# The second self-attention on one ring of double PSUM banks, with its group of heads in another order

## The chip, the cores and the metric

The kernel runs on one core of one Trainium2 chip. The metric is the device time of one execution in microseconds, as the median of several runs. Before the change it is 2383.0 us (three runs: 2380.41, 2383.2 and 2383.0).

## The reference

Two transformer blocks follow each other over x of 8 batches x 512 tokens x 256 channels in float32. The first block has self-attention, cross-attention and a gated feed-forward, all with 16 heads of 16 channels. The second has self-attention with 16 heads of 64 channels, cross-attention to 64 context tokens and a feed-forward with gelu. The change is in the second block's self-attention alone:

```python
def _attn(xq, ctx, wq, wkv, wo, bo):
    q = _heads(xq @ wq)
    k, v = jnp.split(ctx @ wkv, 2, axis=-1)
    ...
    q = _rope(q, sq, cq)
    k = _rope(k, sk, ck)
    sim = jnp.einsum('bhnd,bhmd->bhnm', q, k) * DH ** (-0.5)
    a = jax.nn.softmax(sim, axis=-1)
    o = jnp.einsum('bhnm,bhmd->bhnd', a, v)
    o = o.transpose(0, 2, 1, 3).reshape(xq.shape[0], xq.shape[1], MID)
    return o @ wo + bo
...
attn_in = _adaln(x, cond, ln1_w, ln1_b, g1_w, g1_b, b1_w, b1_b)
x = _attn(attn_in, attn_in, sa_wq, sa_wkv, sa_wo, sa_bo) + x
```

`_rope` multiplies the even and odd channels by a cosine and a sine table and adds or subtracts the products. The 16 heads of 64 channels make 1024 columns for each of q, k and v.

## The kernel before

**Work of a batch.** A batch has 512 tokens. Its normalised rows are transposed into `hT` (two tiles of 128 channels x 512 tokens). Its 16 heads are taken in four groups `g` of four. For a group, `turned` (L999) projects the even and the odd channels of four heads (two products of 128 x 512, each over two slices of 128 channels), multiplies each by the cosine and the sine table on VectorE (L1007, L1008) and lets GpSimd form the rotated even and odd halves (L1010, L1011). It is called for queries and for keys; its products lie in four buffers with the tag `t`, which each call uses all. `values` (L989) projects v for half of the heads (512 columns), tile by tile of 128 tokens.

**Scores and values.** Keys are taken in four tiles of 128 tokens. `score(g, kt)` (L1019) makes the scores of four heads for one key tile, for 512 queries: a head's even and odd halves are 32 rows each, so four heads stand side by side in the array as tiles of 32 rows x 128 columns, and each adds two products. Two double banks take them, and ScalarE makes two tiles `p` of exponentials from them (L1028; six buffers). `value(g, kt)` (L1030) multiplies `p` with v, in tiles of 128 rows x 64 columns, two heads side by side; bank O holds one pair of heads and bank D the other, over the four key tiles. ScalarE copies both to `oT` at the end. The sums of `p` over the key tiles are added up in `sm`: the first addition on GpSimd (L1043) and two more on VectorE (L1047), for each of two pairs of heads. `sums` (L1057) adds `sm` over the partitions with a matrix of ones in tiles of 128 x 32; ScalarE copies the result, and it goes to DRAM and back as `rec`, is inverted on VectorE (`inverse`, L1073), goes to DRAM and comes back spread over the partitions as `rb`. `scaled` (L1090) multiplies `oT` by `rb` on GpSimd. `out_tiles` (L1095) projects the 1024 channels back to 256 and VectorE adds the result to x.

A float32 product is two passes of TensorE in the trace; the profile counts passes.

**PSUM.** Eight banks of 512 float32 columns: two double banks S for scores, one bank O, one bank D, and two banks X for all else. S, O, D and X are rings of their own, so a projection waits for a projection's reader and scores for an exponential.

**Order.** TensorE, VectorE, ScalarE and GpSimd take their instructions in the order in which the Python code issues them (`manual_schedule`). DMAs are issued from SP, in the last group from ScalarE's queue. `slots` (L1152) runs over pairs of key tiles: the scores of an odd key tile, then the jobs listed for this slot (`steps`: projections of the next group or batch, an output projection), the scores of the next even tile, the values of the two tiles before it, then what is listed in `after` (sums, transposes). `mid` puts sums or inverses between jobs. So a group of four key tiles is spread over two slots. After the last group the projections of the cross-attention's values (`cross_values`, L964) run while the last sums go to DRAM and back.

Of the kernel before, what the change touches and what calls it, by code (L numbers as in the profile page):

```python
# [18 lines left out]
P = 128  # L19
# [68 lines left out]
def fast_path(ctx: ExitStack, tc: tile.TileContext, a: dict, out: bass.AP):  # L88
# [7 lines left out]
    psum = ctx.enter_context(tc.tile_pool(name="psum", bufs=2, space=bass.MemoryType.PSUM))  # L96
    turns, extra = [0], []

# [865 lines left out]
    def cross_values(wk, p):  # L964
        ps = bank_x()
        for k in range(2):
            mm(ps, cross["v"][:, k, p * P : (p + 1) * P], ctxzT[:, k, :], k == 0, k == 1)
        v = wk.tile([P, N], F32, tag=f"k{p % 2}", name="v")
        nc.scalar.copy(v, ps)
        nc.sync.dma_start(v_d[:, p], v.rearrange("p (b t) -> p b t", b=B))  # L970


    with tc.tile_pool(name="ph4", bufs=2) as wk:
# [3 lines left out]
        steps, mid, after = {}, {}, {}  # L977

        def last(slot, fn):
            steps.setdefault(slot, []).append(fn)  # L980

        def batch4(b):
            s = {}
            base = 2 * NG * b

            def turn():
                s["hT"] = transposed(nk, s["z"], b, a1, b1, 1)

            def values(half, ts):  # L989
                if ts[0] == 0:  # L990
                    s["v", half] = wk.tile([P, NT, 512], F32, tag="v", name="v")
                for t in ts:
                    ps = bank_x()
                    for k in range(2):
                        mm(ps, s["hT"][:, k, t * P : (t + 1) * P], w_sv[:, k, half * 512 : (half + 1) * 512],
                           k == 0, k == 1)
                    nc.scalar.copy(s["v", half][:, t, :], ps)

            def turned(g, w, tag, pss=None):  # L999

                even, odd = pss or (bank_x(), bank_x())
                for e, ps in enumerate((even, odd)):
                    for k in range(2):
                        mm(ps, w[:, k, (2 * g + e) * P : (2 * g + e + 1) * P], s["hT"][:, k, :], k == 0, k == 1)
                ec, es, oc, os = (wk.tile([P, N], F32, tag="t", name="t", bufs=4) for _ in range(4))
                for ps, c, sn in ((even, ec, es), (odd, oc, os)):
                    nc.vector.tensor_tensor(c, ps, rope_c, ALU.mult)  # L1007
                    nc.vector.tensor_tensor(sn, ps, rope_s, ALU.mult)  # L1008
                s[tag, g] = r = [wk.tile([P, N], F32, tag=f"{tag}{e}", name=f"{tag}{e}") for e in range(2)]
                nc.gpsimd.tensor_tensor(r[0], ec, os, ALU.subtract)  # L1010
                nc.gpsimd.tensor_tensor(r[1], es, oc, ALU.add)  # L1011

            def queries(g, pss=None):
                turned(g, w_sq, "q", pss)

            def keys(g, pss=None):
                turned(g, w_sk, "k", pss)

            def score(g, kt):  # L1019
                pss = [bank_s() for _ in range(2)]  # L1020
                for e in range(2):
                    for j in range(4):
                        r = slice(32 * j, 32 * j + 32)
                        mm(pss[j // 2][:, j % 2, :], s["k", g][e][r, kt * P : (kt + 1) * P], s["q", g][e][r, :],
                           e == 0, e == 1)
                for u in range(2):
                    s["p", g, kt, u] = pr = wk.tile([P, 2, N], F32, tag="p", name="p", bufs=6)
                    nc.scalar.activation(pr, pss[u], AF.Exp, scale=HD1 ** -0.5)  # L1028

            def value(g, kt):  # L1030
                if kt == 0:
                    s["o", 0], s["o", 1] = bank_o(), bank_d()
                for u in range(2):
                    p = 2 * g + u
                    for i in range(2):
                        lo = (p % 4) * P + 64 * i
                        mm(s["o", u][64 * i : 64 * i + 64, :], s["v", p // 4][:, kt, lo : lo + 64],
                           s["p", g, kt, u][:, i, :], kt == 0, kt == NT - 1)

                if kt == 0:  # L1040
                    for u in range(2):
                        s["sm", g, u] = sm = wk.tile([P, 2, N], F32, tag="sm", name="sm", bufs=4)
                        nc.gpsimd.tensor_tensor(sm, s["p", g, 0, u], s["p", g, 1, u], ALU.add)  # L1043
                if kt == 2:
                    for t in (2, 3):
                        for u in range(2):
                            nc.vector.tensor_tensor(s["sm", g, u], s["sm", g, u], s["p", g, t, u], ALU.add)  # L1047
                if kt == NT - 1:
                    for u in range(2):
                        s["oT", 2 * g + u] = o = wk.tile([P, N], F32, tag="oT", name="oT", bufs=10)  # L1050
                        nc.scalar.copy(o, s["o", u])


            def queue(g):
                return nc.scalar if (b, g) == (B - 1, NG - 1) else nc.sync

            def sums(g):  # L1057

                d = bank_x()
# [5 lines left out]
                queue(g).dma_start(dd, den.rearrange("(j r) n -> j r n", j=4)[:, 0, :])  # L1065
                if (b, g) != (B - 1, NG - 1):
                    sums_back(g)

            def sums_back(g):
                s["rec", g] = rec = wk.tile([P, 4 * N // P], F32, tag="rec", name="rec")  # L1070
                queue(g).dma_start(rec, flat(s["dd", g]))

            def inverse(g):  # L1073
                rec = s["rec", g]
                nc.vector.reciprocal(rec, rec)
                s["inv", g] = d = dram.tile([4, N], F32, tag="rec_d", name="rec_d")
                queue(g).dma_start(flat(d), rec)
                check(rec)
                if (b, g) != (B - 1, NG - 1):
                    inverse_back(g)  # L1080

            def inverse_back(g):
                d = s["inv", g]
                for u in range(2):
                    s["rb", g, u] = rb = wk.tile([P, N], F32, tag="rb", name="rb", bufs=3)
                    for e in range(2):
                        queue(g).dma_start(rb[64 * e : 64 * e + 64, :],
                                           d[2 * u + e : 2 * u + e + 1, :].to_broadcast([64, N]))

            def scaled(g, engines=None):  # L1090
                for u, eng in enumerate(engines or [nc.gpsimd] * 2):
                    o = s["oT", 2 * g + u]
                    eng.tensor_tensor(o, o, s["rb", g, u], ALU.mult)  # L1093

            def out_tiles(qp):  # L1095
                project_out(qp, lambda k: s["oT", k], w_so, 8, add_to(b))

            if b:

                pieces = normed_in_pieces(nk, b, EPS1, lambda z: s.update(z=z))  # L1100
                last(base - 8, pieces[0])
                last(base - 6, pieces[1])
                after[base - 6] = [pieces[2]]
                last(base - 5, lambda: add_row(b, row("sabo")))
                after.setdefault(base - 4, []).append(turn)
                last(base - 3, lambda: queries(0))
                last(base - 2, lambda: values(0, (0, 1)))
                last(base - 2, lambda: keys(0))
                last(base - 1, lambda: values(0, (2, 3)))
            else:  # L1110
                s["hT"] = ready

                def begin():
                    queries(0)
                    add_row(0, row("sabo"))
                    both = bank_s()
                    keys(0, (both[:, 0, :], both[:, 1, :]))
                    values(0, (0, 1))

                last(-1, begin)  # L1120

                after[-1] = [lambda: values(0, (2, 3))]
                last(4, lambda: [nc.gpsimd.memset(z, 0.0) for z in (kb, vb)])
                last(5, lambda: load_kb(0))
            for h in range(2):
                last(base + h, lambda h=h: values(1, (2 * h, 2 * h + 1)))
            for g in range(1, NG):
                last(base + 2 * g - 3, lambda g=g: queries(g))
                last(base + 2 * g - 2, lambda g=g: keys(g))
            tail = sums, sums_back, inverse, inverse_back, scaled, out_tiles  # L1130
            return score, value, sums, inverse, scaled, out_tiles, tail

        todo = [batch4(b) for b in range(B)]
# [1154 lines left out]
```

## Time and profile before

| What | Value |
|---|---|
| Median of three runs | 2383.0 us (2380.41 to 2383.2) |
| Span of the profiled execution, first to last instruction | 2378.6 us |
| Own time of the profiled execution outside that span | not listed; the median is 4.4 us above the span |
| Busy in the span: PE, DVE, POOL, ACT | 2361.7, 1141.8, 958.6, 886.8 us |
| Mean granted clock of TensorE | 0.998 |
| Second self-attention: from its first queries to the end of its last output projection | 828.1 to 1815.4 us |
| DVE additions of 128 x 1024 (L1047) | 128, mean 2026 ns, shortest 1211 ns |
| POOL additions of 128 x 1024 (L1043) | 64, mean 2370 ns |
| POOL rotations of queries (L1010, L1011) and of keys | mean 1866 and 2190 ns; 1273 and 1280 ns |
| DVE products with the tables (L1007, L1008), 128 x 512 | mean 690 and 680 ns |
| ACT exponentials of 128 x 1024 (L1028) | 256, mean 1021 ns |

The profile comes from one execution. PE is TensorE's matmul row, PEld its weight loads, which overlap it; DVE is VectorE, ACT ScalarE, POOL GpSimd, SP the queue that issues DMAs. A line of a group or of the timeline names the source line, the operation, the tile written and the tiles read, and the shape; for a matmul 128\*64 means 128 rows x 64 columns of the array. In the timeline the first number is the start and the second the length in us, merged over the instructions counted by x; in brackets stands how long the engine was idle before and who ended that. A matmul's end is modelled, so that matmuls that follow each other overlap a little; the distance of two starts says what a stretch takes.

### The profile page before, as it was taken

Reading aid. Unit: us, or ns where it says so; the run is one execution under the profiler, and the core shown is the slowest. Engines: PE = TensorE matmul, PEld = TensorE weight load, DVE = VectorE, ACT = ScalarE, POOL = GpSimd, SP = SyncE. Lnnn points to the kernel's source line nnn. Section 1 sums busy time; section 2 is a strip of 40 time slices with the busy share of each in tenths; the row PEclk is TensorE's granted clock in tenths of the full one; section 3 lists DMA queues with packets and bytes.
Section 4 is the critical chain, followed back from the end, with each engine's and each line's share of the span. In section 5 each row is a group of like instructions: output and inputs, shape, how many; then the busy total and the mean of one; then the engine's idle time right before and its main releaser. Section 6 shows DMA issues by size and latency. Waiting matters only on the chain.

```text
span 2378.6 us, 28548 instructions
## 1 busy us (share of the span) xinstructions
PE 2361.7 (99%) x10964; PEld 1153.9 (49%) x10964; DVE 1141.8 (48%) x2115; ACT 886.8 (37%) x1118; POOL 958.6 (40%) x588
## 2 busy tenths in 40 slices
PE   9999999999999999999999999999999999999999
PEld 4333544544545633434444444444345566667666
DVE  4564544534335345555454555545445767651110
ACT  4665545555542134333333333333332222221221
POOL 4563223323201046555555555555543545441110
PEclk9999999999999999999999999999999999999999
DMA  5130000000002001000000000000123222210000
GB/s 186 38 104 11 17 15 13 16 15 6 13 11 93 1 1 33 10 26 12 19 19 19 19 19 20 19 19 19 37 59 103 74 65 69 65 59 28 18 23 20
DMA packets 84897, 84.07 MB, mean 35 GB/s; under 512 B 42656, under 2 KB 59792, under 8 KB 84752
## 3 DMA queue, kind: packets, MB, share of 16 engines
q1 hardware_dynamic: 83208, 78.99, 10.8%
q8 instruction: 88, 1.44, 0.2%
q0 software_dynamic: 640, 2.10, 0.2%
q10 hardware_dynamic: 904, 1.07, 0.1%
q14 instruction: 57, 0.47, 0.1%
HBM read 72.09 MB, written 10.04 MB: 35 GB/s over the span
## 4 chain that ended last, share of the span: by engine, by line
PE 96%; DMA 1%; DVE 1%; issue 1%; ACT 1%; POOL 0%; SPq 0%; DVEq 0%; ACTq 0%; POOLq 0%
PE ps_X L118 39%; PE ps_S L118 24%; PE ps_D L118 16%; PE ps_O L118 14%; PE ps_X L429 1%; DMA rb<-rec 1%; PE ps_X L616 1%; PE ps_X L576 0%; ACT p L596 0%; DMA rec<-rec 0%; PE ps_D L616 0%; PE ps_D L429 0%; POOL var L567 0%; PE ps_D L576 0%; ACT den L1063 0%
## 5 line engine op out<-in xcount | busy, mean ns | idle before, releaser
L118 PE MATMUL ps_S<-q,k 32*128 32x512 f32 (+1 forms) x3072 | 416.3, 622 | 2.5 <-ACT p L596 1.5
L1028 ACT ACTIVATE p<-ps_S 128x1024 f32<-128x1024 f32 x256 | 248.4, 1021 | 449.5 <-PE ps_S L118 449.2
L596 ACT ACTIVATE p<-ps_S 128x1024 f32<-128x1024 f32 x256 | 248.2, 1022 | 197.5 <-PE ps_S L118 196.8
L118 PEld LDWEIGHTS ps_S<-q,k 32*128 32x128 f32 (+1 forms) x3072 | 141.5, 183 | 228.0 <-issue 161.5
L1047 DVE TENSOR_TENSOR sm<-sm,p 128x1024 f32<-128x1024 f32 x128 | 251.8, 2026 | 0.3 <-issue 0.2
L1010 POOL TENSOR_TENSOR q<-t 128x512 f32<-128x512 f32 x32 | 59.7, 1866 | 327.8 <-DVE t L1008 286.8
L1007 DVE TENSOR_TENSOR t<-ps_X,rope_c 128x512 f32<-128x512 f32 x126 | 86.9, 690 | 211.2 <-PE ps_X L118 211.2
L184 POOL TENSOR_TENSOR rstd<-rstd,mhalf 128x4 f32<-128x4 f32 x49 | 50.1, 1023 | 329.4 <-DVE rstd L183 328.1
L853 POOL TENSOR_TENSOR q<-t,t 128x512 f32<-128x512 f32 x72 | 94.9, 1318 | 154.8 <-DVE t L852 151.7
L567 POOL TENSOR_TENSOR var<-var,mhalf 128x32 f32<-128x32 f32 (+1 forms) x17 | 87.4, 5140 | 170.1 <-DVE var L561 169.9
L1043 POOL TENSOR_TENSOR sm<-p 128x1024 f32<-128x1024 f32 x64 | 149.9, 2370 | 1.8 <-ACT p L1028 1.8
L118 PE MATMUL ps_X<-hT,w 128*128 128x512 f32 x328 | 150.5, 597 | 0.0
L1093 POOL TENSOR_TENSOR oT<-oT,rb 128x512 f32<-128x512 f32 x63 | 126.7, 2029 | 29.2 <-DMA rb<-rec_d 29.2
L118 PE MATMUL ps_O<-p,v 128*64 128x512 f32 x512 | 134.9, 605 | 0.0
L118 PE MATMUL ps_D<-p,v 128*64 128x512 f32 x512 | 131.6, 592 | 0.0
L118 PE MATMUL ps_O<-p,h 128*32 128x512 f32 x1024 | 130.4, 610 | 0.8 <-ACT p L596 0.8
L118 PE MATMUL ps_X<-w_sa_wv,hT 128*128 128x512 f32 x256 | 118.3, 605 | 0.0
L118 PE MATMUL ps_X<-hT,w_sa_wq 128*128 128x512 f32 x256 | 115.9, 595 | 0.0
L118 PE MATMUL ps_X<-w_sa_wo,oT 128*128 128x256 f32 x512 | 113.9, 381 | 0.6 <-DVE t L1008 0.5
L118 PE MATMUL ps_X<-hT,w_sa_wk 128*128 128x512 f32 x248 | 113.2, 599 | 0.0
L118 PE MATMUL ps_S<-hT,w_ff_w 128*128 128x512 f32 x256 | 111.3, 592 | 0.0
L466 DVE TENSOR_TENSOR x<-ps_X,x 128x512 f32<-128x512 f32 x27 | 18.7, 691 | 190.5 <-PE ps_X L118 190.5
(283 smaller groups left out, 3619.4 us busy)
## 6 DMA issues: line engine op xcount, KB each, us to landing
rb<-rec SPq DMA_DIRECT2D x128, 128.0 KB
rb<-rec_d SPq DMA_DIRECT2D x124, 128.0 KB
rb<-rec SPq DMA_DIRECT2D x16, 256.0 KB
out_dram<-x SPq DMA_DIRECT2D x15, 256.0 KB
x<-in_x_dram SPq DMA_DIRECT2D x7, 512.0 KB
gate<-modd SPq DMA_DIRECT2D x24, 128.0 KB
k_d<-q POOLq DMA_DIRECT2D x8, 256.0 KB, 2.4
v_d<-v SPq DMA_DIRECT2D x8, 256.0 KB
```

Of the source, the lines that this page charges most:

```text
L118: nc.tensor.matmul(o, lhsT, rhs, start=start, stop=stop)
L184: nc.gpsimd.tensor_tensor(r[:, :n], r[:, :n], mhalf[:, :n], ALU.pow)
L429: nc.tensor.transpose(ps[:, t * P : (t + 1) * P], z[:, t, k * P : (k + 1) * P], ident)
L567: nc.gpsimd.tensor_tensor(var, var, half, ALU.pow)
L596: nc.scalar.activation(pr[u], pss[u], AF.Exp, scale=HD0 ** -0.5)
L853: nc.gpsimd.tensor_tensor(dst, t1, t2, ALU.add)
L1007: nc.vector.tensor_tensor(c, ps, rope_c, ALU.mult)
L1010: nc.gpsimd.tensor_tensor(r[0], ec, os, ALU.subtract)
L1028: nc.scalar.activation(pr, pss[u], AF.Exp, scale=HD1 ** -0.5)
L1043: nc.gpsimd.tensor_tensor(sm, s["p", g, 0, u], s["p", g, 1, u], ALU.add)
L1047: nc.vector.tensor_tensor(s["sm", g, u], s["sm", g, u], s["p", g, t, u], ALU.add)
L1093: eng.tensor_tensor(o, o, s["rb", g, u], ALU.mult)
```

## The change

PSUM becomes, for this stage, one ring of four double banks (tag `pair`), used by everything in turn; before and after the stage the pool is closed and opened again (`other_banks`). The schedule by slots goes. A group now is: scores of key tiles 0 and 1, all of its jobs, scores of key tiles 2 and 3, values of all four tiles, sums. The jobs are queries and keys of the next group; in group 1 also the output projection of the last batch, in group 2 the second half of the values before them and the transposes of the next batch behind them, in group 3 values, queries and keys of the next batch.

Further edits: queries and keys are projected into one double bank and VectorE takes 1024 columns at once, with the table repeated; `t` has two buffers of the double size. `values` fills a double bank with two tiles, which ScalarE copies at once. Values are computed in tiles of 128 x 32 (twice the instructions) into one double bank for both pairs of heads, copied at once. The additions to `sm` (`add`) are made for one pair of heads on VectorE and for the other on GpSimd, each right behind its scores. `scaled` uses VectorE for one pair and GpSimd for the other. The output projection of a batch is one piece in one double bank with one addition to x. The transposes and the projections of the cross-attention's values use double banks too. `p` keeps six buffers.

The diff, cut to its core (`s` is a batch's dictionary):

```diff
+    def other_banks():
+        nonlocal psum
+        banks.close()
+        psum = banks.enter_context(tc.tile_pool(name="psum", bufs=2, space=bass.MemoryType.PSUM))
+
+    def pair():
+        return psum.tile([P, 2, 512], F32, tag="pair", name="ps_P", bufs=4)
...
-            def turned(g, w, tag, pss=None):
-                even, odd = pss or (bank_x(), bank_x())
-                for e, ps in enumerate((even, odd)):
...
-                ec, es, oc, os = (wk.tile([P, N], F32, tag="t", name="t", bufs=4) for _ in range(4))
-                for ps, c, sn in ((even, ec, es), (odd, oc, os)):
-                    nc.vector.tensor_tensor(c, ps, rope_c, ALU.mult)
-                    nc.vector.tensor_tensor(sn, ps, rope_s, ALU.mult)
+            def turned(self, g, w, tag):
+                s = self.s
+                ps = pair()
+                for e in range(2):
+                    for k in range(2):
+                        mm(ps[:, e, :], w[:, k, (2 * g + e) * P : (2 * g + e + 1) * P], s["hT"][:, k, :], k == 0, k == 1)
+                c, sn = (wk.tile([P, 2, N], F32, tag="t", name="t") for _ in range(2))
+                nc.vector.tensor_tensor(c, ps, rope_c[:, None, :].to_broadcast([P, 2, N]), ALU.mult)
+                nc.vector.tensor_tensor(sn, ps, rope_s[:, None, :].to_broadcast([P, 2, N]), ALU.mult)
                 s[tag, g] = r = [wk.tile([P, N], F32, tag=f"{tag}{e}", name=f"{tag}{e}") for e in range(2)]
-                nc.gpsimd.tensor_tensor(r[0], ec, os, ALU.subtract)
-                nc.gpsimd.tensor_tensor(r[1], es, oc, ALU.add)
+                nc.gpsimd.tensor_tensor(r[0], c[:, 0, :], sn[:, 1, :], ALU.subtract)
+                nc.gpsimd.tensor_tensor(r[1], sn[:, 0, :], c[:, 1, :], ALU.add)
...
-                pss = [bank_s() for _ in range(2)]
+                pss = [pair() for _ in range(2)]
...
+            def add(self, g, kt):
+                s = self.s
+                for u, eng in enumerate((nc.vector, nc.gpsimd)):
+                    if kt == 1:
+                        s["sm", g, u] = wk.tile([P, 2, N], F32, tag="sm", name="sm", bufs=4)
+                        eng.tensor_tensor(s["sm", g, u], s["p", g, 0, u], s["p", g, 1, u], ALU.add)
+                    else:
+                        eng.tensor_tensor(s["sm", g, u], s["sm", g, u], s["p", g, kt, u], ALU.add)
...
+            def value(self, g):
+                s = self.s
+                ps = pair()
+                for kt in range(NT):
                     for u in range(2):
+                        p = 2 * g + u
+                        for i in range(2):
+                            for h in range(2):
+                                lo = (p % 4) * P + 64 * i + 32 * h
+                                r = slice(64 * i + 32 * h, 64 * i + 32 * h + 32)
+                                mm(ps[r, u, :], s["v", p // 4][:, kt, lo : lo + 32], s["p", g, kt, u][:, i, :],
+                                   kt == 0, kt == NT - 1)
+                s["oT", g] = o = wk.tile([P, 2, N], F32, tag="oT", name="oT", bufs=5)
+                nc.scalar.copy(o, ps)
...
-                d = bank_x()
+                d = pair()[:, 0, :]
...
+            def out(self):
+                ps = pair()
+                o = [self.s["oT", k // 2][:, k % 2, :] for k in range(8)]
+                for t in range(NT):
+                    project_tile(ps[:, t // 2, :], t % 2, lambda k: o[k], w_so, 8, t)
+                x = xs[self.b]
+                nc.vector.tensor_tensor(x, ps.rearrange("p i (j d) -> p (i j) d", j=2), x, ALU.add)
...
+                for g in range(NG):
+                    for kt in range(2):
+                        this.score(g, kt)
+                    this.add(g, 1)
+                    jobs = [lambda: this.queries(g + 1), lambda: this.keys(g + 1)] if g < 3 else []
+                    if g == 1 and last:
+                        jobs.append(last.out)
+                    if g == 2:
+                        jobs = [lambda: this.values(1)] + jobs + ([nxt.turn] if nxt else [])
+                    if g == 3 and nxt:
+                        jobs = [lambda: nxt.values(0), lambda: nxt.queries(0), lambda: nxt.keys(0)]
+                    for n, fn in enumerate(jobs):
+                        fn()
+                        if n == 0 and before:
+                            before[0].inverse(before[1])
+                        if n == 0 and nxt and g == 0:
+                            nxt.norm(0)
...
+                    for kt in (2, 3):
+                        this.score(g, kt)
+                        this.add(g, kt)
+                    this.value(g)
+                    if nxt and g < 2:
+                        nxt.norm(g + 1)
+                    if before:
+                        before[0].scaled(before[1])
+                    this.sums(g)
+                    before = this, g
```

## The prediction

> **What bounds the kernel now.** I read the page first, then the order of TensorE's work in the second self-attention, then the same 30 us with every engine. The page's shares of engines and its chain:
>
> ```profile
> PE 2361.7 (99%) x10964; PEld 1153.9 (49%) x10964; DVE 1141.8 (48%) x2115; ACT 886.8 (37%) x1118; POOL 958.6 (40%) x588
> ...
> PE 96%; DMA 1%; DVE 1%; issue 1%; ACT 1%; POOL 0%; SPq 0%; DVEq 0%; ACTq 0%; POOLq 0%
> ```
>
> TensorE (PE) never rests and is the chain: only less time on PE helps, and every new wait of PE counts in full. One group of four heads, PE alone:
>
> ```profile
> 1300.45 1.03 PE L118 MATMUL ps_D<-p,v 128*64 128x512 f32 x4
> 1301.31 1.03 PE L118 MATMUL ps_O<-p,v 128*64 128x512 f32 x4
> ...
> 1303.13 1.07 PE L118 MATMUL ps_X<-sm,ones 128*32 128x512 f32 x8
> 1304.12 2.00 PE L118 MATMUL ps_S<-q,k 32*128 32x512 f32 x16
> 1306.05 3.70 PE L118 MATMUL ps_X<-w_sa_wv,hT 128*128 128x512 f32 x8
> 1309.59 3.60 PE L118 MATMUL ps_X<-hT,w_sa_wq 128*128 128x512 f32 x8
> 1313.12 2.00 PE L118 MATMUL ps_S<-q,k 32*128 32x512 f32 x16
> 1315.05 1.08 PE L118 MATMUL ps_O<-p,v 128*64 128x512 f32 x4
> ```
>
> Read start to start. Four passes of values, two side by side, take 0.86 us (1300.45 to 1301.31): a pass is 0.43, 0.428 finely. A key tile of scores, 16 passes four side by side, needs 1.71 and takes 1.93: 0.22 over. A block of projections: 16 passes need 6.85, take 7.07: 0.22. Values (1315.05 to the next scores at 1318.63): 3.58 for 3.43, 0.15. Sums: 0.99 for 0.86, 0.13. Nothing else is lost in this stretch: there is no wait for data in it. Then what stands beside it on VectorE (DVE) and GpSimd (POOL):
>
> ```profile
> 1313.30 0.69 DVE L1007 TENSOR_TENSOR t<-ps_X,rope_c 128x512 f32<-128x512 f32 x1 [0.43 <-PE ps_X L118]
> 1313.90 0.68 DVE L1008 TENSOR_TENSOR t<-ps_X,rope_s 128x512 f32<-128x512 f32 x1
> ...
> 1314.50 7.86 DVE L1047 TENSOR_TENSOR sm<-sm,p 128x1024 f32<-128x1024 f32 x4
> 1314.75 2.10 POOL L1010 TENSOR_TENSOR q<-t 128x512 f32<-128x512 f32 x1 [8.41 <-DVE t L1008]
> ...
> 1316.81 2.25 POOL L1011 TENSOR_TENSOR q<-t 128x512 f32<-128x512 f32 x1
> ```
>
> A POOL addition of 512 columns takes 2.10 here, but 1.27 where DVE is quiet; a DVE addition of 1024 takes 7.86/4 = 1.97, at its shortest 1.21. The ends interleave one by one (POOL ends 1316.85 and 1319.06): they take turns.
>
> **What the Trainium skill says.** "TensorEngine Tiling (Array Packing)", Key Properties: changing the tiling mode drains the TensorE. The trace agrees: the excess of 0.13 to 0.22 sits at changes of tile, and adjoining projections of one tile add none. "SBUF — State Buffer", Who interferes with whom: a DVE instruction with two SBUF inputs contends with a GpSimd one that reads SBUF, while one with at most one SBUF input doesn't. The trace agrees twice: the turns above, and rope products (one input from PSUM), which keep their 0.68 to 0.69. "TensorE: Matmul & The Clock Gate", Part 1: an idle window of about 3.4 us halves the clock. It is seen here twice at 0.50, for 71.5 to 74.9 and 92.0 to 95.4 us; in this stage it stays at 1.00.
>
> **The change, part by part.**
>
> *Fewer changes of tile.* A group had 4 score stretches, 2 blocks of projections, 2 stretches of values and sums: 4 x 0.22 + 2 x 0.22 + 2 x 0.15 + 0.13 = 1.75 us of drains. After: 2 score stretches of two key tiles, 1 block, 1 stretch of values, and sums of the same 128x32 tile behind it: 2 x 0.22 + 0.22 + 0.15 = 0.81. Saved 0.94 x 32 groups = **30 us**, all on PE.
>
> *Values in 32 columns.* Twice the instructions, four side by side instead of two: 64 x 0.428 / 4 = 6.85, as before (32 / 2 x 0.428). The first self-attention's values have this form and need 1.85 for 16 passes, drain included, so nought. If weight loads (0.109 against 0.43 / 4 = 0.107) got in the way, 0.1 us a group at most: 0 to 3.
>
> *ScalarE.* One copy of 1024 replaces two of 512 for oT and v; exps stay. ACT is 37% busy: nought. The probabilities keep six buffers where values now come after all four key tiles (eight tiles): the exps of tile 3 wait for the values of tile 0. Values start 0.15 after the scores, need 0.86 per key tile and half, so tile 0's first half is done at 1.0, its exp (1.02) at 2.1, and tile 3 is wanted at 0.15 + 5.14 = 5.3: hidden, with 3 us to spare.
>
> *The ring.* Every PSUM tile now comes in turn from four double banks. In a group with queries and keys as its last jobs the order is: scores 0 and 1 (A B C D), queries A, keys B, scores 2 (C D), scores 3 (A B), values C, sums D. So scores 3 wait for the **rope products of the keys just projected**; before, scores had four banks of their own. And those products wait: `t` has two buffers, both held by the queries until POOL has formed q. From PE's end of queries: to DVE 0.18 (1313.12 to 1313.30); two products of 1024 from PSUM, not shown before: an SBUF pair of 1024 takes 1.21 alone, consecutive starts overlap by 0.08, so 2.34 (ends: 2.2, and twice two of 512, 2.7); to POOL 0.12; q even and odd 2.48 (1.27 each, at 833.36 to 835.84 in the trace); 0.04; the keys' two products 2.34; back to PE 0.08. Sum 7.58. PE has, from the same point: keys 3.43, the half of the block's 0.22 that lies at its end 0.10, scores 2 1.93 = 5.46. **PE waits 2.1 us** (1.7 to 2.9). Behind it on PE's queue are half of scores 3, values, sums and all later groups. Where: group 0 of 8 batches, group 1 of the first batch (it has no output projection), group 3 of 7 batches, group 2 of the last: 17 places, 36 us. In group 2 of the other seven the transposes (1.36) follow the keys: 0.8 x 7 = 6. In group 1 of seven batches the output projection (14 us) covers it.
>
> *Sums.* Before, DVE added four of the six sums and POOL two (L1047, L1043); now each has three, and the last two of POOL follow the keys' rotation. From the end of the keys' products, in turns: DVE 1.15, POOL k 1.2 and 1.2, POOL addition 2.34 (4.67 for two), DVE 1.15, POOL 2.34 = 9.4. PE from there: 0.08, scores 3 1.71, drain 0.15, values 6.85 = 8.8. PE waits about 0.5 (0 if they didn't contend, 7.2; 1.3 if DVE's scaling, 0.69, gets in too) at the same 24 places: 12 us.
>
> *Moved steps.* The inverse (reciprocal 0.25, two checks 0.24) and, in group 0, half the norm (1.04) come between the products of queries and keys on DVE: 1.5 of the 2.6 us in which DVE waits for POOL's q, so nought; with no such wait they would cost up to that. Their DMAs (rec, rec_d, four rb on SP) stand in the same order and come back within 8 us (reciprocal 1779, second factor 1786.2) against about 15 until scaling. Scaling is shared by DVE and POOL after the last addition: it delays no sum. The row addition on POOL precedes scaling at group 1's end, with group 2's values of 7 us as cover; without it 2.4.
>
> *Ends.* The last group of all has no jobs: scores 2 and 3 wait for exps at 0.97 each, 0.7 us. The output of the last batch is added in one DVE piece of 1024 (1.2), and the next stage's first bank is released by it: 1.5 us. At the start keys' rotation follows queries' and a row addition on POOL and ends within 0.2 us of the values: nought (0 to 1).
>
> Sum: 36 + 6 + 12 + 0.7 + 1.5 - 30 = **+26 us**. On the span of 2378.6 it makes 2404.6; the median of the runs is 4.4 above that span (2383.0), the rest lies around it and stays: **2409**.
>
> **Rivals.**
> (a) *Faster*: the ring's wait is covered, drains alone remain: 2383 - 30 + 2 = 2355. It turns where the wait per place falls below (30 - 2) / 24 = 1.2 us, against my 2.3. The mechanism would be PE work that is longer, or a rotation on POOL that is shorter, than read; against it, 1.27 each is also the distance of POOL's starts, and DVE did restart at 835.88, just behind it. Between them, at 1.0 to 1.4 a place, lies no change.
> (b) *The clock falls*: a stall of 2.1 us, half of scores 3 running in it, lies in one 3.4-us window about a third of the time. The halved windows of before came just after stalled scores; against it, 78.3 to 81.7 had PE busy 1.95 of 3.40 and kept 1.00. Each halved window costs 1.7: eight give 2423, all 24 give 2450.
> (c) *32-column values are slower than 0.43 a pass*: 3 us by the loads above, inside my range.
>
> **How the numbers follow.** Forecast 0.62, (a) 0.16, no change between 0.07, (b) 0.15. The forecast's own range, from waits of 1.7 to 2.9 and sums of 0 to 1.3, is 2387 to 2446 (17 x 1.7 + 7 x 0.4 and no wait of sums, or 17 x 2.9 + 7 x 1.6 + 24 x 1.3). The range 2376 to 2446 takes in no change and most of (b), and leaves out (a) and the worst of (b). Faster and slower count from 0.2%, about what a measurement of this kernel tells from no change: faster 0.16, same 0.07, slower 0.77.
>
> **What would show it.** Right: PE idle before scores of tile 3, released by DVE's rope product, some 2 us in groups 0 and 3; DVE's keys waiting for POOL; scores stretches of two tiles at 3.64; values with sums at 7.9 without a drain between; about 0.5 us before sums, released by POOL. Wrong: those waits under a microsecond, a values stretch well over 7, or a lowered clock in the stage.

## The result and the profile after

The changed kernel takes 2421.56 us (median of four runs, 2416.05 to 2422.95) against 2381.7 for the kernel before (four runs, 2380.36 to 2383.2): 1.0164 times as long, 95% interval 1.0151 to 1.0177. That is 39.9 us slower, where 26 were forecast. The profiled execution took 2421.05 us, with a span of 2419.3.

First the page of the changed kernel: the busy row and the chain of work that ended last.

```profile
PE 2363.9 (98%) x11988; PEld 1171.5 (48%) x11988; DVE 1088.9 (45%) x1978; ACT 874.4 (36%) x1054; POOL 960.0 (40%) x589
...
PE 88%; DVE 5%; POOL 3%; issue 1%; DMA 1%; ACT 1%; SPq 0%; ACTq 0%; DVEq 0%; POOLq 0%
```

PE is busy for 2.2 us more than before in all. What changed is the chain: PE falls from 96% to 88%, and DVE (from 1%) and POOL (from 0%) have 8% together. PE now stands and waits for them. PE's timeline over group 0 of a batch and the start of group 1 shows the places:

```profile
1335.63 3.72 PE L128 MATMUL ps_P<-q,k 32*128 32x512 f32 x32
1339.28 3.70 PE L128 MATMUL ps_P<-hT,w_sa_wq 128*128 128x512 f32 x8
1342.81 3.60 PE L128 MATMUL ps_P<-hT,w_sa_wk 128*128 128x512 f32 x8
1346.34 2.85 PE L128 MATMUL ps_P<-q,k 32*128 32x512 f32 x20
1350.61 1.99 PE L128 MATMUL ps_P<-q,k 32*128 32x512 f32 x12 [1.42 <-DVE t L1035]
1352.52 7.08 PE L128 MATMUL ps_P<-p,v 128*32 128x512 f32 x64
1359.41 1.28 PE L128 MATMUL ps_P<-sm,ones 128*32 128x512 f32 x8
1360.62 3.72 PE L128 MATMUL ps_P<-q,k 32*128 32x512 f32 x32
```

Start to start: scores of key tiles 0 and 1 take 3.65 (1335.63 to 1339.28), 0.22 over their 3.43, so one drain for two tiles. Values take 6.89 for 6.85: 32 columns cost nothing, and the drain behind them, before the sums of the same tile, is gone too. But scores of tiles 2 and 3 take 6.18 (1346.34 to 1352.52) where 3.65 would do: 2.53 lost, and the bracket names the rope product of DVE as what ended the wait. Sums take 1.21 where the next group needs 0.97: 0.24 lost. All engines over the same stretch show the chain behind the wait:

```profile
1343.08 1.22 DVE L1034 TENSOR_TENSOR t<-ps_P,rope_c 128x1024 f32<-128x1024 f32 x1 [1.25 <-PE ps_P L128]
...
1345.58 1.27 POOL L1037 TENSOR_TENSOR q<-t 128x512 f32<-128x512 f32 x1 [1.54 <-DVE t L1035]
...
1346.81 1.27 POOL L1038 TENSOR_TENSOR q<-t 128x512 f32<-128x512 f32 x1
...
1348.11 1.22 DVE L1034 TENSOR_TENSOR t<-ps_P,rope_c 128x1024 f32<-128x1024 f32 x1 [1.35 <-POOL q L1038]
...
1349.25 1.21 DVE L1035 TENSOR_TENSOR t<-ps_P,rope_s 128x1024 f32<-128x1024 f32 x1
```

It is the chain of the forecast, step by step: two products for the queries, two rotations on POOL that free `t`, two products for the keys (whose projections PE had done at 1346.34), and then PE at 1350.61. The bracket there counts 1.42 only, because PE had begun the part of tile 3 whose bank was free, and the modelled ends of its passes reach into the wait; the loss is read from the starts. The three largest kinds of wait of PE listed from 828 to 1860 us (total, times, longest):

```profile
PE ps_P L128 <- DVE t L1035: 26.2, 24, 1.4
PE ps_P L996 <- ACT hT L997: 7.0, 8, 1.0
PE ps_P L128 <- ACT v L980: 3.7, 4, 1.7
```

The first row has the 24 places of the forecast: by the starts 17 of them lose 2.53 each and seven, in group 2, 0.58. The second and third were not in it. They are the transposes and the values of the cross-attention, of which PE's timeline shows this:

```profile
1289.28 0.60 PE L996 MATMUL ps_P<-ident,z 128*128 128x128 f32 x4
1290.75 0.66 PE L996 MATMUL ps_P<-ident,z 128*128 128x128 f32 x4 [0.87 <-ACT hT L997]
1291.34 2.00 PE L128 MATMUL ps_P<-q,k 32*128 32x512 f32 x16
1293.64 2.00 PE L128 MATMUL ps_P<-q,k 32*128 32x512 f32 x16 [0.31 <-DVE t L1035]
```

The code transposes one half into a double bank, lets ScalarE read it, and transposes the other half into the same double bank. With two single banks the second half did not wait, in the transposes or in the values of the cross-attention; now it starts only after ScalarE's read of the first. The same two pieces of work in the kernel before, each without a gap:

```profile
1786.02 14.00 PE L118 MATMUL ps_X<-ctxzT,w_ca_wvp 96*128 96x512 f32 x32
1799.97 1.42 PE L429 MATMUL ps_X<-ident,z 128*128 128x128 f32 x8
```

**The account.** From the first queries to the first instruction of the next stage, start to start, PE takes 987.3 us before and 1022.9 after: 35.6 more. The passes themselves, at 0.428 us per 512 columns and as many side by side as the tiles allow, are 925.2 in both, so 62.1 before and 97.7 after is excess. By kind of stretch:

| Stretch | excess before, us | after, us | of it after |
|---|---|---|---|
| scores | 28.1 | 61.7 | drains 13.9; waits 17 x 2.53, 7 x 0.58, last group 0.7 |
| projections of q, k, v | 11.6 | 5.7 | drains |
| values | 10.4 | 1.2 | drains |
| sums | 5.0 | 11.6 | drains 3.5; waits 8.1: about 0.27 x 23, 1.3 in group 1 of the first batch, last group 0.4 |
| transposes | 4.2 | 9.6 | 5.4 more than before, at 8 places |
| values of the cross-attention | 0.3 | 4.9 | 4.6 more, at 4 places |
| output projections | 2.5 | 3.0 | the wait for the last addition to x 1.36 |

The rest of the 40.7 by which the spans differ lies outside the stage: 4.2 ahead of it and 0.8 behind. Ahead of it the first block, which the change doesn't touch, had its clock halved for 13.6 us in this execution against 6.8 in the one before, and the first pair of the new pool waits 0.56. How often the clock is halved there varies between executions of one kernel, so some 3 us of the difference (half of the 6.8 more) aren't the change's. In the changed stage the clock stayed at 1.00 in both profiles.

### The profile page after: what moved, and what is told of

Same layout as the page of the kernel before. It is cut to its first block, busy times and chain, and to the rows that moved or that the text cites. A ratio compares the mean times of both kernels' runs of the same rounds, so it can differ in the third digit from the quotient of the medians.

```text
span 2419.3 us, 30288 instructions
## 1 busy us (share of the span) xinstructions
PE 2363.9 (98%) x11988; PEld 1171.5 (48%) x11988; DVE 1088.9 (45%) x1978; ACT 874.4 (36%) x1054; POOL 960.0 (40%) x589
## 4 chain that ended last, share of the span: by engine, by line
PE 88%; DVE 5%; POOL 3%; issue 1%; DMA 1%; ACT 1%; SPq 0%; ACTq 0%; DVEq 0%; POOLq 0%
PE ps_P L128 34%; PE ps_X L128 20%; PE ps_S L128 13%; PE ps_D L128 9%; PE ps_O L128 9%; DVE t L1034 2%; DVE t L1035 2%; POOL q L1037 1%; POOL q L1038 1%; DMA rb<-rec 1%; PE ps_X L439 1%; PE ps_X L626 1%; PE ps_X L586 0%; ACT p L606 0%; PE ps_D L439 0%
## 5 line engine op out<-in xcount | busy, mean ns | idle before, releaser
L1056 ACT ACTIVATE p<-ps_P 128x1024 f32<-128x1024 f32 x256 | 244.8, 1026 | 393.9 <-PE ps_P L128 393.9
L606 ACT ACTIVATE p<-ps_S 128x1024 f32<-128x1024 f32 x256 | 248.2, 1022 | 200.8 <-PE ps_S L128 200.1
L128 PE MATMUL ps_P<-q,k 32*128 32x512 f32 x2048 | 259.2, 605 | 26.2 <-DVE t L1035 26.2
L128 PE MATMUL ps_P<-p,v 128*32 128x512 f32 x2048 | 226.4, 594 | 0.0
L1065 POOL TENSOR_TENSOR sm<-sm,p 128x1024 f32<-128x1024 f32 x64 | 178.3, 2785 | 82.8 <-ACT p L1056 80.8
L128 PE MATMUL ps_S<-q,k 16*128 16x512 f32 x1024 | 161.5, 645 | 2.5 <-ACT p L606 1.5
L1065 DVE TENSOR_TENSOR sm<-sm,p 128x1024 f32<-128x1024 f32 x64 | 120.6, 1885 | 96.0 <-ACT p L1056 96.0
L128 PE MATMUL ps_P<-hT,w_sa_wq 128*128 128x512 f32 x256 | 116.8, 599 | 0.6 <-issue 0.6
L128 PE MATMUL ps_P<-hT,w_sa_wk 128*128 128x512 f32 x256 | 115.1, 592 | 0.0
L128 PE MATMUL ps_P<-w_sa_wv,hT 128*128 128x512 f32 x256 | 114.0, 598 | 0.0
```

The costliest lines, as they stand in the source:

```text
L128: nc.tensor.matmul(o, lhsT, rhs, start=start, stop=stop)
L606: nc.scalar.activation(pr[u], pss[u], AF.Exp, scale=HD0 ** -0.5)
L1065: eng.tensor_tensor(s["sm", g, u], s["sm", g, u], s["p", g, kt, u], ALU.add)
```

## The experiments

All medians stand beside runs of the kernel before on the same chip: 2380.61 us for the first four kernels, 2381.38 for the last three. "Stage" is the stretch of 1022.9 us above, read from each kernel's own trace. A median compared with the changed kernel's 2421.56 comes from another set of runs; the kernel before differs between the sets by 1.1 us at most.

| Kernel | median, us | ratio to before, 95% interval | stage, us |
|---|---|---|---|
| changed kernel (in its own runs) | 2421.56 | 1.0164 (1.0151 to 1.0177) | 1022.9 |
| four buffers of `t` | 2387.76 | 1.0033 (1.0023 to 1.0044) | 991.8 |
| values behind the keys | 2393.63 | 1.0047 (1.0029 to 1.0065) | 1000.4 |
| last addition on VectorE | 2416.41 | 1.0150 (1.0124 to 1.0176) | 1020.2 |
| both halves, then ScalarE | 2413.96 | 1.0133 (1.0107 to 1.0160) | 1017.0 |
| three repairs together | 2360.58 | 0.9903 (0.9886 to 0.9921) | 961.8 |
| eight buffers of `p` | 2431.47 | 1.0210 (1.0190 to 1.0230) | 1037.4 |
| before, values in 32 columns | 2376.13 | 0.9979 (0.9971 to 0.9987) | 982.3 |

### Four buffers of t

Theory: scores wait for the keys' products because those wait for POOL to free `t`. Rivals: they wait for something else, or the lost time is the clock's. The room is taken from `sm`, which needs two buffers.

```diff
-                c, sn = (wk.tile([P, 2, N], F32, tag="t", name="t") for _ in range(2))
+                c, sn = (wk.tile([P, 2, N], F32, tag="t", name="t", bufs=4) for _ in range(2))
...
-                        s["sm", g, u] = wk.tile([P, 2, N], F32, tag="sm", name="sm", bufs=4)
+                        s["sm", g, u] = wk.tile([P, 2, N], F32, tag="sm", name="sm", bufs=2)
```

> The products with the rope tables get four buffers t in place of two (and sm two in place of four, to make room; by the order of the program no addition waits for that). If the keys' products wait on GpSimd's rotation of the queries, they now start when the projection of the keys ends: 0.27 + 2.36 + 0.15 behind it, against 1.93 + 0.10 of TensorE, so a wait of 0.9 per place is left (1.6 in group 0, where the inverse and half a norm stand before them), of 2.5 before. That is 8 x 0.9 + 9 x 1.6 + 7 x 0.3 = 24 us less than the changed kernel's 2421.6: about 2397. If it is the ring alone, with VectorE's two products as the long piece: no change, 2421.

Measured: 2387.76, 33.8 less than the changed kernel, and 31.1 less in the stage, more than the 24 expected. One group 0 with every engine:

```profile
1326.58 4.80 PE L128 MATMUL ps_P<-q,k 32*128 32x512 f32 x32
...
1326.91 1.21 DVE L1034 TENSOR_TENSOR t<-ps_P,rope_c 128x1024 f32<-128x1024 f32 x1
1326.99 1.27 POOL L1038 TENSOR_TENSOR q<-t 128x512 f32<-128x512 f32 x1
...
1331.31 7.07 PE L128 MATMUL ps_P<-p,v 128*32 128x512 f32 x64
```

The keys' product now starts at 1326.91, ahead of POOL's second rotation, and not 0.03 behind its end as in the changed kernel. The two tiles of scores take 4.73 (1326.58 to 1331.31) for 3.65: 1.08 lost here and at five other places in group 0, 0.95 at the other 11 of the 17, where it had been 2.53; the seven places in group 2 lose nothing. The excess of all scores falls from 61.7 to 31.5. So 30 of the 48 us that scores waited come from the two buffers of `t`. What stays, 0.95 to 1.08 a place, is the ring alone: the keys' two products (2.35) and the two handovers (0.27 and 0.15) make 2.77, and PE has 1.81 of its own in that time. I had expected 1.6 in group 0 for the inverse and half the norm that DVE has to do between the products; they took 1.4 and ended just as the keys came, so that they cost the 0.13 between 0.95 and 1.08.

### Values behind the keys

Without a change of buffers, the same wait should be covered by PE work whose reader is quick. Values are read by ScalarE with one copy, so they are put between the keys and the scores in groups 2 and 3.

```diff
-                        jobs = [lambda: this.values(1)] + jobs + ([nxt.turn] if nxt else [])
+                        jobs = jobs + [lambda: this.values(1)] + ([nxt.turn] if nxt else [])
                     if g == 3 and nxt:
-                        jobs = [lambda: nxt.values(0), lambda: nxt.queries(0), lambda: nxt.keys(0)]
+                        jobs = [lambda: nxt.queries(0), lambda: nxt.keys(0), lambda: nxt.values(0)]
```

> Group 3 projects queries, keys and then values of the next batch, and group 2 queries, keys, values and then the transposes; group 0 stays as it is. By my theory 6.9 us of values then stand between the keys and the scores, and cover the rope products: the waits of 2.5 us in group 3 (7 places) and in the last batch's group 2, the 0.3 of the other groups 2, and the 0.35 of the sums in both groups go: 17.7 + 2.5 + 2.2 + 15 x 0.35 = 28 us, 2394. Group 0 keeps its 2.5. If the waits come from the exponentials or from the ring being too short for any order, they stay or move to the values' copies: 2415 to 2425.

Measured: 2393.63. PE in a group 3:

```profile
1302.05 7.03 PE L128 MATMUL ps_P<-w_sa_wv,hT 128*128 128x512 f32 x16
1309.01 3.72 PE L128 MATMUL ps_P<-q,k 32*128 32x512 f32 x32
1312.65 7.07 PE L128 MATMUL ps_P<-p,v 128*32 128x512 f32 x64
1319.54 1.04 PE L128 MATMUL ps_P<-sm,ones 128*32 128x512 f32 x8
```

Behind the keys stand the values. The scores then take 3.64, without a wait, and the sums 0.98 (next scores at 1320.52): with the rotation out of the way earlier, POOL's last addition is in time as well. The wait for DVE falls from 26.2 at 24 places to 12.7 at 9, those of group 0 and the one in the first batch. One thing was not expected: the transposes' wait rose from 7.0 to 10.3, since ScalarE now has the copy of the values ahead of them. In the stage the kernel is 22.5 us shorter than the changed one, not 28: besides those 3.3 a stretch of 6.8 us at half clock near the stage's end (from 1810.3) costs this execution 2.7 in the last transposes and output projections. That the median met the expected 2394 to the microsecond is in part luck.

### The last addition on VectorE

Sums wait for POOL's last addition. If DVE makes that one, the wait should go.

```diff
-                for u, eng in enumerate((nc.vector, nc.gpsimd)):
+                for u, eng in enumerate((nc.vector, nc.vector if kt == 3 else nc.gpsimd)):
```

> The addition of key tile 3 is made on VectorE for both pairs of heads, so GpSimd's last long addition no longer stands before the sums. If the sums wait for GpSimd, their stretch falls from 1.2 to about 0.97 where it waits (24 places), 8 us in all: 2414. If the excess of the sums is only a drain of TensorE, or VectorE's additions are then the late ones: 2421 or more.

Measured: 2416.41, and 2.7 less in the stage; 1.6 more would be gone but for a stretch of 3.4 us at half clock in this execution (from 1828.7). The excess of the sums falls by 3.1 of the 8 us expected, from 11.6 to 8.5. In group 0 the wait is gone in all batches but the last, and so are the 1.3 in group 1 of the first batch, but in groups 2 and 3 it stayed. Every engine at such a place:

```profile
1416.15 4.94 DVE L1065 TENSOR_TENSOR sm<-sm,p 128x1024 f32<-128x1024 f32 x2 [1.84 <-ACT p L1056]
1417.74 2.26 POOL L1123 TENSOR_TENSOR oT<-oT,rb 128x512 f32<-128x512 f32 x1
...
1420.85 1.34 PE L128 MATMUL ps_P<-sm,ones 128*32 128x512 f32 x8
```

POOL, relieved of the addition, begins its scaling at 1417.74, in the middle of DVE's two additions, which take 4.94 instead of the 2.4 of two alone; the first of them also ran beside POOL's addition of key tile 2, which ended at 1417.78. The load was moved and the sharing stayed.

### Both halves, then ScalarE

The second half of a double bank is written before ScalarE reads the first, for the transposes and the cross-attention's values.

```diff
             for k in range(2):
                 for t in range(NT):
                     nc.tensor.transpose(ps[:, k, t * P : (t + 1) * P], z[:, t, k * P : (k + 1) * P], ident)
+            for k in range(2):
                 nc.scalar.activation(hT[:, k, :], ps[:, k, :], AF.Identity, bias=b1[:, k, b : b + 1], scale=a1[:, k, b : b + 1])
...
                 mm(ps[:, p % 2, :], cross["v"][:, k, p * P : (p + 1) * P], ctxzT[:, k, :], k == 0, k == 1)
+        for p in (2 * pp, 2 * pp + 1):
             v = wk.tile([P, N], F32, tag=f"k{p % 2}", name="v")
```

> In a double bank of transposes, and of projections of the cross-attention's values, both halves are issued on TensorE before ScalarE reads the first. If TensorE waited there because a half being read holds the whole double bank: 0.9 less at 8 places of transposes and 4.6 at the projections. In seven of those places the wait for the keys' products takes over (0.3 becomes 1.2), so only 0.9 + 4.6 = 5.5 us are gained: 2416. If each of those waits counted by itself: 11.8 us, 2410. If the wait was for ScalarE's queue: no change.

Measured: 2413.96, and 5.9 less in the stage. Both kinds of wait are gone from the list. The excess of the transposes falls from 9.6 to 0.8, even below the 4.2 of before, and that of the cross-attention's values from 4.9 to 0.1. But 6.9 came back in scores: in group 2 the transposes had covered the rope products, and shorter transposes cover less (0.58 lost a place became 1.6). A wait that hides another is worth only the difference.

### Three repairs together

Four buffers of `t`, both halves ahead of ScalarE, and the values as the cover wherever the ring was late: the second half of them goes to group 0, behind the keys, and in group 3 they follow the keys too.

```diff
+                    if g == 0:
+                        jobs = jobs + [lambda: this.values(1)]
                     if g == 2:
-                        jobs = [lambda: this.values(1)] + jobs + ([nxt.turn] if nxt else [])
+                        jobs = jobs + ([nxt.turn] if nxt else [])
                     if g == 3 and nxt:
-                        jobs = [lambda: nxt.values(0), lambda: nxt.queries(0), lambda: nxt.keys(0)]
+                        jobs = [lambda: nxt.queries(0), lambda: nxt.keys(0), lambda: nxt.values(0)]
```

> What the first experiments point to, together: four buffers t (and two sm), the second half of the values behind the keys of group 0, the next batch's values behind its keys in group 3, and both halves of a double bank issued before the first is read. If the waits behind the keys' products, the sums behind them and the half-read double banks are all that the change costs, only the drains are left: 63 score stretches at 0.22, 32 of values and sums at 0.15, projections about 9, and waits of about 5 at the first batch's group 1, the last group and the last addition to x. That is 31 us above the passes' own 925, where the kernel before stood 62 above them: 2350 from 2380.6. If something else of the ring costs time as well (exponentials that queue behind the values' copies, say), it shows as score stretches above 3.65 in groups 0 and 3, and the time lies between 2360 and 2385.

Measured: 2360.58, faster than both kernels. PE in group 0:

```profile
1316.77 7.03 PE L128 MATMUL ps_P<-w_sa_wv,hT 128*128 128x512 f32 x16
1323.73 3.72 PE L128 MATMUL ps_P<-q,k 32*128 32x512 f32 x32
1327.38 7.07 PE L128 MATMUL ps_P<-p,v 128*32 128x512 f32 x64
```

The values follow the keys' projections, and from there to the sums nothing waits: scores take 3.65, values 6.89. The stage's excess is 36.6, against 62.1 before: this is what fewer changes of tile bring when the ring is covered (3.4 of the difference are the transposes, which now lose less than before). The time is 10 us above what I expected. The stage has 5.6 of these, 36.6 where I had 31: sums still lose 0.4 at nine places and 1.3 in group 1 of the first batch, and two score stretches lose 1.0 each, of which only a part was in my 31. The rest is that this execution's stage began 5 us later than that of before, 3.4 of it by a further stretch of 6.8 us at half clock in the first block.

### Eight buffers of p

The forecast cost the six buffers of `p` at nothing. With eight, no exponential waits for values; the room is again taken from `sm`, of which two buffers did no harm in the kernel with four of `t` (excess of its sums 10.7).

```diff
-                    s["p", g, kt, u] = pr = wk.tile([P, 2, N], F32, tag="p", name="p", bufs=6)
+                    s["p", g, kt, u] = pr = wk.tile([P, 2, N], F32, tag="p", name="p", bufs=8)
...
-                        s["sm", g, u] = wk.tile([P, 2, N], F32, tag="sm", name="sm", bufs=4)
+                        s["sm", g, u] = wk.tile([P, 2, N], F32, tag="sm", name="sm", bufs=2)
```

> Probabilities p get eight buffers in place of six (sm two in place of four to make room), so that the exponentials of key tile 3 no longer wait for the values of key tile 0. By my forecast that wait was hidden: no change from 2421, and at most 3 us less, if the earlier additions let the sums start without their 0.3. If the six buffers cost TensorE time, the stretches of values get shorter than 6.89 and the time falls by more than 5 us.

Measured: 2431.47, 10 us slower than the changed kernel, which neither theory had. Values take 6.89 as before, so the six buffers do cost PE nothing. But the sums lose more, 21.2 us of excess instead of 11.6. DVE and POOL ahead of one of them:

```profile
1359.61 6.20 POOL L1065 TENSOR_TENSOR sm<-sm,p 128x1024 f32<-128x1024 f32 x2
...
1361.65 1.35 DVE L193 TENSOR_SCALAR rstd<-mv 128x4 f32<-128x4 f32 x1
1362.91 0.68 DVE L1123 TENSOR_TENSOR oT<-oT,rb 128x512 f32<-128x512 f32 x1
1365.11 1.82 PE L128 MATMUL ps_P<-sm,ones 128*32 128x512 f32 x8
```

And POOL's two additions at the same place in the changed kernel:

```profile
1353.91 5.68 POOL L1065 TENSOR_TENSOR sm<-sm,p 128x1024 f32<-128x1024 f32 x2
```

Exponentials of tile 3 come earlier, so DVE begins its last addition 1.06 ahead of POOL's two (at 1358.55), where it had been 0.80 behind their start, and goes on earlier to the norm and the scaling. In the changed kernel the step L193 of the norm took 1.33 and ended with POOL's second addition, and the scaling (L1123) began at 1359.53, 0.06 before POOL's end. Now L193 ends with POOL's first addition, and the scaling falls into the second. POOL's additions start as long after the values' start as in the changed kernel (1.39) but take 6.20 instead of 5.68, and POOL's is the addition that sums wait for. The rest of the stage's 14.5 lies in two stretches of 6.8 us at half clock that this execution has (from 950.3 and 1848.0). The medians too are 10 us apart, but the mean clock is lower here in the other runs as well (0.994 to 0.996, against 0.996 to 0.999 for the changed kernel), and how much of their 10 us is the clock's was not separated.

### Before, with values in 32 columns

This is rival (c) by itself: the kernel before, with nothing changed but the tile of the values.

```diff
-                        lo = (p % 4) * P + 64 * i
-                        mm(s["o", u][64 * i : 64 * i + 64, :], s["v", p // 4][:, kt, lo : lo + 64],
-                           s["p", g, kt, u][:, i, :], kt == 0, kt == NT - 1)
+                        for h in range(2):
+                            lo = (p % 4) * P + 64 * i + 32 * h
+                            r = slice(64 * i + 32 * h, 64 * i + 32 * h + 32)
+                            mm(s["o", u][r, :], s["v", p // 4][:, kt, lo : lo + 32],
+                               s["p", g, kt, u][:, i, :], kt == 0, kt == NT - 1)
```

> The kernel before with one part of the change alone: values in tiles of 32 columns, four side by side, in their old two stretches. If the drains are paid at changes of tile, the sums that follow values lose theirs: 0.30 for a stretch of values and the sums behind it becomes 0.15, at about 28 places: 4 us less than 2380.6. If tiles of 32 columns are slower than 64 because four weight loads of 0.11 us do not fit into a pass of 0.43, values take 0.1 us more in each of 64 stretches: 2383 to 2387.

Measured: 2376.13, 5.3 us less than before, and 5.0 less in the stage. PE from values to sums:

```profile
1298.10 1.06 PE L118 MATMUL ps_O<-p,v 128*32 128x512 f32 x8
...
1301.55 1.04 PE L118 MATMUL ps_X<-sm,ones 128*32 128x512 f32 x8
```

Values that stand before sums take 3.45 (1298.10 to 1301.55) for 3.43, where the 64 columns had 3.58; values before scores keep 3.57. The excess of all values falls from 10.4 to 6.1 us, that of the sums from 5.0 to 4.3. Four tiles of 32 columns run at the rate of two of 64, and the sums' tile, of the same shape, follows without a drain.

## Why the prediction was right in direction and short in size

**Drains.** Forecast 30 saved; measured 30.9 (scores 14, values and sums 10, projections 6, output projections 1). "TensorEngine Tiling (Array Packing)", Key Properties, on which this step rested, is borne out: the excess went with the changes of tile, and where values and sums share a tile only 0.04 is left between them.

**The ring.** The mechanism and its 24 places were right. The 17 places were put at 2.1 us each and cost 2.53, 43 instead of 36. Half of the 0.43 is the chain: it takes 7.80 from PE's end of queries (1342.81 to 1350.61), not 7.58, since PE to DVE is 0.27 (0.18 was read from a product of 512) and DVE to PE 0.15 (0.08). The other half is an error in "scores 2 1.93 = 5.46": that has a drain in it, but between two tiles of scores there is none, and the one drain of the stretch had been counted in the first step. PE has 3.53 for the keys and 1.71 for scores 2, 5.24 in all, and 7.80 - 5.24 = 2.56. The pair of products of 1024 columns was put at 2.34 and took 2.36. Group 2 was put at 6 and cost 4, because the transposes took longer than counted; without their own wait it is 1.6 a place, 11 in all, as the fourth experiment shows. That `t` is the link was shown by its two extra buffers: 30 us back.

**Sums.** Forecast 12; measured 8.1: some 0.3 instead of 0.5 at 23 of the 24 places, 1.3 at the other, and 0.4 in the last group, which the forecast had at nothing. The way of reckoning, instruction by instruction in turns, was right: from the end of the keys' products to the end of POOL's last addition it gave 9.4, and the trace has 9.1 (1350.46 to 1359.59). The 1.3 is in group 1 of the first batch, where POOL first clears two tiles (L1168 and L1169, 0.95 each, at 889.47 and 890.36) and only then adds; the forecast doesn't name these. "SBUF — State Buffer", Who interferes with whom, says who shares, and the third and the sixth experiment show what follows from it: which engine does an addition matters less than what the other one does at that moment. The page's sentence on a DVE instruction with at most one SBUF input excepts the 2-port modes, which the prediction left out: L193 has one input in SBUF and was held up all the same (1.33 and 1.35 for 0.17). In which mode it ran, no run here shows.

**What failed: "In group 2 of the other seven the transposes (1.36) follow the keys", and the silence on the cross-attention's values.** That a tile of two banks is handed over as one was known for the ring and not applied to the transposes and values of the cross-attention, where the code writes one half, reads it, and writes the other. This cost 5.4 and 4.6 us, 10 of the 13.9 us between forecast and result; it also covered 2 of group 2's wait. Code that got another tile, but no other order, was read as unchanged.

**Costed at nothing.** Values in 32 columns: right (6.89; rival (c) is refuted by the last experiment). Six buffers of `p`: right for PE; with eight the sums lost 9.6 more. Inverse and norm between the products: right, DVE still had 1.35 us idle before the keys' product. The first pair of the pool: 0.56 instead of 0. (The last addition to x, put at 1.5, cost 1.36.)

**Rivals.** (a), the wait covered, did not happen, and its price was fair: with the cover put in by hand the kernel takes 2360.58, where (a) had 2355. (b), a clock halved by the stalls, is not in the stage of the changed kernel, but it was near. In three other kernels the stage has four halved stretches: from 1810.3 with values behind the keys, from 1828.7 with the last addition on VectorE, from 950.3 and 1848.0 with eight buffers of `p`. In the 3.40 us ahead of each of them PE is listed busy for only 1.70 to 1.81. In the changed kernel's stage the least busy such window, counted in steps of 3.413 us from its halved stretch at 80.9, has 1.97 (1473.6 to 1477.0), and the clock stayed; one of 1.88 with four buffers of `t` (1798.4 to 1801.8) kept it too. So what a stall does seems to depend on how it falls into these windows. It is not a rule: in the kernel before, the halved stretches at 71.5 and 92.0 follow windows with PE listed busy for 2.83 of 3.40 and for all of 3.50 us. The prediction's "It is seen here twice" therefore holds for the halved clock, not for an idle window ahead of it.

**The sum.** Forecast +26. Add 10 for the halves, 7 for the places, take 2 for group 2, 4 for the sums and 1 for the drains: +36, the stage's 35.6. Of the remaining 4 of the 39.9, the profiled executions put some 3 down to the clock of the first block, which isn't the change's.

**Left open.** Why the clock is halved in some executions and places of the first block and not in others, and whether the stalls alone halve it in the stage. A split of the last addition to x, and a ring that leaves scores their own banks, were not tried.

## What to carry to other kernels

One ring in program order ties every user to the reader of the tile that had the same bank before it, here four places back: list, for each tile, who reads it last and what PE has to do until the ring comes round, and put work with a quick reader behind work with a slow one. The buffers between that reader's steps belong to the chain as much as the PSUM banks; two more of them were worth 31 us here, as much as all the drains saved. When two banks become one tile, look through all users for code that fills one half, reads it and then fills the other.

## What the runs showed of the hardware

- Four column tiles of 32 run beside each other at the rate of two of 64 (6.89 us a group for 6.85 of passes), and a following stretch of the same tile starts without a drain; two tiles of scores behind each other have none between them either.
- A small DVE instruction can be held up by POOL: the step on 128 x 4 elements (L193) takes 0.17 at its shortest, and 1.33 and 1.35 where POOL adds two tiles from SBUF. Both times it ended 0.03 us behind one of POOL's additions (1359.61 for 1359.59, 1363.00 for 1362.97).
- The halved clock comes on a grid: within each of the nine traces every halved stretch begins a whole number of steps of 3.413 us behind the first (with eight buffers of `p`, 515 steps from 90.2 to 1848.0), and those that end before the kernel does are one, two or three steps long.
- Giving exponentials more buffers, so that nothing waits for them, cost the sums 9.6 us: VectorE, being earlier, ran into the additions on GpSimd for which the sums wait.
